# A graph attention and GCN kernel: first quotients, early loads, last stores and the last result block rearranged at the change of stage

## The chip, the core and the metric

The kernel runs on one core of one Trainium2 chip. The metric is device time in microseconds of one execution of the whole program. Engines are called as in the profile: PE is TensorE (PEld its weight loads), DVE is VectorE, ACT is ScalarE, POOL is GpSimd, and SP issues most of the transfers. A name with q behind it (SPq, ACTq, POOLq) is that engine's queue when it issues a transfer. All data is float32.

## What is computed

Two layers on N = 2708 nodes with D = 128 features and an adjacency matrix adj of 2708 x 2708. The first is an attention with 8 channels per score and one head per feature, in which the adjacency is added to the scores twice:

```
q, k, v = (x @ W.T).reshape(d, n, h)          # h = 8, d = 128 heads
a   = softmax(q @ k.T * scale + adj + adj)    # for each of the 128 heads, 2708 x 2708
out = (a @ v).reshape(n, h * d) @ Wo.T
x   = layernorm(x + out)
```

The second is a graph convolution with a residual path:

```
hidden = adj @ (x @ W2) + b2
cross  = adj @ (hidden @ W4) + b4
x      = layernorm(x + cross + hidden @ res_w.T + res_b)
```

## The kernel before

**Attention.** The 128 heads are worked in 32 groups g of four. In a group the 2708 query columns are cut into six blocks b of 452 columns (the last has 448; `QBS`), and a block has nine steps i (`plan`). In a step, TensorE forms scores of keys against queries (line 447) into PSUM; VectorE adds the adjacency to most of them (`add_near`, line 454), and ScalarE takes the exponential (line 557). For a third of the tiles ScalarE takes the exponential of the bare scores (line 554) and GpSimd multiplies it with a stored exponential of the adjacency (line 555). TensorE then multiplies the exponentials with the values (`add_up`, lines 464 to 472) and collects nine rows per head: eight weighted sums and the sum of the weights. Those sums trail the scores by several steps. When a block's sums are complete, `hand_on` copies them out of PSUM on VectorE (line 478) and stores them to the DRAM tile `os` in four transfers (line 481), issued by SP, and for the very last block by ScalarE.

**Order.** The order of all engines is written out by hand. A planner, `interleave`, holds the cost of each piece of work and decides which of scores, sums and copies comes next; it yields one item at a time, and the loop of lines 492 to 557 emits it. SP issues the adjacency tiles in that order, some eight loads ahead. At the beginning of a step (c == 0) the loop also emits what belongs to the next group or to the next stage. In the last group, from block 1 on, that is one of six `early` loads per step (line 525): the output weights `wo`, the first 128 rows of the transposed adjacency `near0`, the first 128 rows of sums `ot0`, and `x0`, `w2` and `w4`. In the last block it is the quotient of `ot0` by its sum of weights: the reciprocal ahead of step 3 (line 529), the multiplication ahead of step 5 (line 531). In the last group `look_at_near` (line 436) adds a reduction on VectorE in three of the nine steps, the last step among them.

**The second stage, `finish`.** It begins when the attention's memory is free. GpSimd sets a few tiles (lines 602 and 603). Then 22 chunks c of 128 nodes (the last has 20) pass through: `divide` (quotients on VectorE; for chunk 0 only the reductions of line 628, since its quotients are there), `turn` (four transposes on TensorE, line 634, and a copy by ScalarE, line 636, twice), `mix` (products with `wo`, line 642), `add_x` (addition, statistics, root on ScalarE, scaling, lines 647 to 653), and `spread` (line 659), which multiplies the new features with whole rows of the adjacency, two chunks later. `load` (ot and xt) and `load_rows` (rows) fetch a few chunks ahead through SP. Ahead of the loop ScalarE's queue issues four small loads (line 677): rw and the three vectors b. After the loop come `hidden`, `hidden_values`, `collect` (lines 718 to 744) and for each of six column blocks `results` (lines 753 to 775): transposes, addition to the features, statistics, root, scaling and the store. The last column block has 148 columns: one part of 128 rows and one of 20, worked one after the other. `judge` looks whether all sums stayed in range; a branch at the end repeats the attention with row maxima if they did not.

**Completion of transfers.** Transfers issued by SP and ScalarE are counted on eight semaphores in turn. A transfer that gets a semaphore waits on its own queue until the transfer eight places before it in that turn has landed. The turn is shared by both queues.

Of the kernel before, what the change touches and what calls it, by code (L numbers as in the profile page):

```python
# [9 lines left out]
F32 = mybir.dt.float32  # L10
F32R = mybir.dt.float32r
I32 = mybir.dt.int32
AF = mybir.ActivationFunctionType
# [5 lines left out]
P = 128  # L19
H = 8  # L20
GB = 4
NB = 512
QB = 452
# [119 lines left out]
def graph_attention_gcn(ctx: ExitStack, tc: tile.TileContext, x, xT, adj, adjT, adjP, adjS,  # L143
# [10 lines left out]
    nc = tc.nc  # L154
    N, D = x.shape
    R = N * D
    NG = D // GB
# [3 lines left out]
    QBS = chunks(N, QB)  # L161
# [9 lines left out]
    const = ctx.enter_context(tc.tile_pool(name="const", bufs=1))  # L171
# [17 lines left out]
    wo = const.tile([P, H, D], F32, name="wo")  # L189
    w2, w4 = (const.tile([P, P], F32, name=f"w{i}") for i in range(2))  # L190
    near0 = const.tile([P, N], F32, name="near0")
    ot0 = const.tile([P, H + 1, P], F32, name="ot0")
    x0 = const.tile([P, D], F32, name="x0")
    o3 = os_.rearrange("e (i g) -> i e g", g=P)
    early = [(wo.rearrange("g e f -> g (e f)"), WoT), (near0, adjT[:P, :]), (ot0, o3[:P]), (x0, x[:P, :]), (w2, W2), (w4, W4)]
    assert 2 * GB * N >= P * P

    with ExitStack() as s:
# [233 lines left out]
        def look_at_near(g, b, m):  # L432

            x = TWO_EXP.index(m)
            if x % 3 == g - NG + 3:
                nc.vector.tensor_reduce(ends[:, 0, ds(b * len(TWO_EXP) + x, 1)], exp_cols[g, b, m][:, : QBS[b][1]],
                                        AX.X, ALU.min)
# [37 lines left out]
        def hand_on(g, b):  # L475
            n0, nw = QBS[b]
            o = opool.tile([P, QB], F32, tag="o", name="o")
            nc.vector.tensor_copy(o[:, :nw], acc.pop((g, b))[:, :nw])  # L478
            queue = nc.scalar if (g, b) == (NG - 1, len(QBS) - 1) else nc.sync
            for j in range(GB):  # L480
                queue.dma_start(os_[:, ds((GB * g + j) * N + n0, nw)], o[ds(32 * j, H + 1), :nw])

# [9 lines left out]
        for what, n, c, beside in interleave(plan, len(steps) // len(plan), NU, amid, bufs=5):  # L492
            if what == "amid":
                at = amid.index(n)
                jobs += project(at)
                continue
            if what == "add_up":
                g, b = divmod(n, len(QBS))
                add_up(g, b, c, where.pop((g, b, c)))
                continue  # L500
            if what == "hand_on":
                hand_on(*divmod(n, len(QBS)))
                continue
            g, b, i = steps[n]
            pieces, two, _ = plan[i]
            nw = QBS[b][1]
            if c == 1 and jobs:
                jobs.pop(0)()
            if c == 0:
                nq = (g, b + 1) if b + 1 < len(QBS) else (g + 1, 0)  # L510
                if i == 3 and nq[0] < NG:
                    load_q(*nq)

                if g + 1 < NG:
                    t = b * len(plan) + i
                    if t < 32 and t % 2 == 0:
                        load_keys(g + 1, t // 2)
                    elif t < 32 and t % 8 == 7:
                        load_values(g + 1, t // 8)
                    elif 33 <= t < 50 and t % 2:  # L520
                        order_keys(g + 1, (t - 33) // 2)
                    elif t >= 50:
                        spread_values(g + 1, t - 50)
                if g == NG - 1 and b and early:
                    nc.sync.dma_start(*early.pop(0))
                if (g, b) == (NG - 1, len(QBS) - 1) and i in (3, 5):
                    if i == 3:
                        quotient = opool.tile([P, QB], F32, tag="o", name="o")[:, :P]
                        nc.vector.reciprocal(quotient, ot0[:, H, :])
                    else:  # L530
                        nc.vector.tensor_mul(ot0[:, :H, :], ot0[:, :H, :], quotient.unsqueeze(1).to_broadcast([P, H, P]))
                last = max(loads.index((g, b, x), max(0, loaded - 40)) for x in [chunks_of(p) for p in pieces] + [-1 - two])
                while loaded < min(len(loads), last + 1 + ahead):
                    load_adj(loaded)
                    loaded += 1
                e = epool.tile([P, 8, QB], F32, tag="e", name="e")
                sp = pq.tile([P, 3, NB], F32, tag="p", name="p")
                w = ppool.tile([P, 3, QB], F32, tag="w", name="w")
                if g == 0:
                    first_exp(b, two)  # L540
                at = k = 0
            st = ps.tile([P, 2, NB], F32, tag="s", name="s")
            for r, (m, j) in enumerate(pieces[c]):
                score(st[:, r], g, b, m, j)
                where.setdefault((g, b, m), {})[j] = e, at + r
            for j in beside:
                score(sp[:, k], g, b, two, j)
                where.setdefault((g, b, two), {})[j] = w, k
                k += 1
            add_near(e, st, g, b, pieces[c], at)  # L550
            at += 2
            if c == len(pieces) - 1:
                look_at_near(g, b, two)
                nc.scalar.activation(w[:, :, :nw], sp[:, :, :nw], AF.Exp, scale=2.0)  # L554
                nc.gpsimd.tensor_mul(w[:, :, :nw], w[:, :, :nw],  # L555
                                     exp_cols[g, b, two][:, :nw].unsqueeze(1).to_broadcast([P, 3, nw]))
                nc.scalar.activation(e[:, :at, :nw], e[:, :at, :nw], AF.Exp, scale=2.0)  # L557
# [3 lines left out]
    stat = ctx.enter_context(tc.tile_pool(name="stat", bufs=4))  # L561

    rw = keep.tile([P, P], F32, name="rw")
    b2_sb, b4_sb, rb_sb, bias = (keep.tile([P, 1], F32, name=f"b{i}") for i in range(4))
    eps = keep.tile([P, 1], F32, name="eps")
    n_fine = keep.tile([1, 1], I32, name="n_fine")

# [14 lines left out]
    def finish(s):  # L582
# [90 lines left out]
        for c in (1, 2):  # L673
            load(c)
            load_rows(c)
        for t, a in ((rw, res_wT), (b2_sb, b2), (b4_sb, b4), (rb_sb, res_b)):
            nc.scalar.dma_start(t, a)
        nrow = 3
        for c in range(NM):
            if c + 3 < NM:  # L680
                load(c + 3)
            while nrow < NM and nrow <= min(c + 4, max(c + NR - 2, NR)):
                load_rows(nrow)
                nrow += 1
            if c == 1:
                spread(0, range(NK))
            turn(c, 0)
            if c > 2:
                spread(c - 2, range(3))
            turn(c, 1)  # L690
            if c > 2:
                spread(c - 2, range(3, NK))
            mix(c)
            if c == 0:
                add_x(0)
            if c + 1 < NM:
                divide(c + 1)
            if c == 0:
                divide(0)
            else:  # L700
                add_x(c)
# [51 lines left out]
        def results(k):  # L753
            n0, nw = NBS[k]
            cs, eT = block_chunks[k], embeds.pop(k)
            pe = turned.tile([P, 4, P], F32, tag="pt", name="pe")
            for c in cs:
                m0, mw = MC[c]
                nc.tensor.transpose(pe[:mw, c - cs[0], :], eT[:, ds(m0 - n0, mw)], ident)
            y, o = (two.tile([P, 4, D], F32, tag=t, name=t) for t in ("y4", "o4"))  # L760
            mv = stat.tile([P, 4, nc.vector.BN_AGGR_DIM], F32, tag="mv4", name="mv4")
            full = len([c for c in cs if MC[c][1] == P])
            parts = [(0, full, P)] + [(c - cs[0], 1, MC[c][1]) for c in cs[full:]]
            for i, n, w in parts:
                nc.vector.tensor_add(y[:w, ds(i, n), :], pe[:w, ds(i, n), :], x1[:w, ds(cs[0] + i, n), :])
                for r in range(i, i + n):
                    statistics(mv[:w, r, :], y[:w, r, :], w)
                sd, rs = (stat.tile([P, 4], F32, tag=t, name=t) for t in ("sd4", "rs4"))
                nc.scalar.activation(sd[:w, :n], mv[:w, ds(i, n), 1], AF.Sqrt, bias=eps[:w])
                nc.vector.reciprocal(rs[:w, :n], sd[:w, :n])  # L770
                for r in range(i, i + n):
                    nc.vector.tensor_scalar(o[:w, r, :], y[:w, r, :], mv[:w, r, 0:1], rs[:w, r - i : r - i + 1],
                                            ALU.subtract, ALU.mult)
                m0 = MC[cs[0] + i][0]
                nc.sync.dma_start(out[ds(m0, n * w), :].rearrange("(c p) f -> p c f", p=w), o[:w, ds(i, n), :])

        def judge():
            fine = one.tile([P, 5], F32, name="fine")
# [316 lines left out]
```

## Time and profile before

| what | us |
|---|---|
| three runs | 6856.6, 6847.54, 6854.3; median 6854.3 |
| the profiled execution | 6854.41 |
| its span, first to last instruction | 6852.6 |
| attention, until the last copy of sums (line 478) | 6541.05 |
| from there until the first sums of line 659 begin | 14.9 |
| last scaling on VectorE ends | 6847.1 |
| busy PE, DVE, ACT, POOL | 6636.6, 6114.5, 6503.0, 5789.9 |
| mean granted TensorE clock | 0.992 |

The profiled execution lies 0.1 us from the median, and its own time is 1.8 us more than its span. Busy shares are means over stages with different limits. Stretches of some microseconds are therefore read in three views: the timeline of one engine (start, duration, engine, line, operation, output and input, and in brackets the idle time before it and what ended it), the windows view (busy time of each engine in a stretch, and the granted TensorE clock as a share of full speed), and the chain of waits, which runs back from the last instruction through what released each step.

### The profile page before, as it was taken

To read this page: it belongs to the slowest core of one execution; us is meant where nothing else is said; L and a number is where in the kernel's file an instruction comes from. 1 tells how busy PE (TensorE), PEld (TensorE's weight loads), DVE (VectorE), ACT (ScalarE), POOL (GpSimd) and SP (SyncE) were. 2 spreads that over 40 slices of the span, in tenths; PEclk is the share of its full clock that TensorE was granted. 3 is DMA by queue.
4 is the path that set the end of the run, shared out by engine and by line. 5 is a ranking of instruction groups with operands and counts; after the bars stand their busy time and mean duration, and the time that the engine had idled before them with its cause. 6 is when DMAs were issued, how large, how long until landed. Compare 5 with 4: busy or idle time off the path is not lost.

```text
span 6852.6 us, 138413 instructions
## 1 busy us (share of the span) xinstructions
PE 6636.6 (97%) x50612; PEld 1985.7 (29%) x50612; DVE 6114.5 (89%) x6368; ACT 6503.0 (95%) x3660; POOL 5789.9 (84%) x2706
## 2 busy tenths in 40 slices
PE   7999999999999999999999999999999999999999
PEld 2222222222222222222222222222222222222254
DVE  6899999999999999999999999999999999999952
ACT  7999999999999999999999999999999999999920
POOL 5898988999988999989899899899998888888810
PEclk8999999999999999999999999999999999999999
DMA  8888888888888888888888888888888887777774
GB/s 245 268 248 251 255 244 240 249 244 246 249 248 253 243 252 250 249 244 248 247 247 249 246 257 248 251 244 245 245 250 243 243 245 232 229 231 227 232 252 131
DMA packets 1147712, 1665.68 MB, mean 243 GB/s; under 512 B 151376, under 2 KB 1129852, under 8 KB 1140220
## 3 DMA queue, kind: packets, MB, share of 16 engines
q1 hardware_dynamic: 1146120, 1655.82, 79.8%
q8 instruction: 401, 6.57, 0.4%
q14 instruction: 287, 2.35, 0.1%
q10 hardware_dynamic: 904, 0.94, 0.1%
HBM read 1574.37 MB, written 81.80 MB: 242 GB/s over the span
## 4 chain that ended last, share of the span: by engine, by line
PE 51%; DMA 11%; DVE 10%; POOL 9%; issue 7%; ACT 6%; SPq 6%; DVEq 0%; POOLq 0%; ACTq 0%
PE acc L472 25%; PE s L447 16%; DVE e L454 9%; POOL w L555 8%; SPq L296 3%; ACT e L557 3%; DMA col<-in_adjP 3%; DMA two<-in_adjP 3%; ACT w L554 2%; DMA ecol<-ne 2%; PE acc L464 2%; PE p L447 2%; PE acc L659 2%; PE acc L741 2%; PE s L353 1%
## 5 line engine op out<-in xcount | busy, mean ns | idle before, releaser
L555 POOL TENSOR_TENSOR w<-w,ecol 128x1356 f32<-128x1356 f32 (+1 forms) x1728 | 5348.2, 3102 | 689.4 <-ACT w L554 624.2
L454 DVE TENSOR_TENSOR e<-s,col 128x904 f32<-128x904 f32 (+1 forms) x4608 | 4816.7, 1092 | 316.0 <-PE s L447 78.2
L557 ACT ACTIVATE e<-e 128x2712 f32<-128x2712 f32 (+5 forms) x1728 | 4637.0, 2683 | 16.7 <-DVE e L454 11.3
L472 PE MATMUL acc<-e,vals 128*9 128x452 f32 x20352 | 3565.4, 546 | 0.0
L447 PE MATMUL s<-q,k 32*128 32x452 f32 x10944 | 2495.9, 461 | 123.5 <-DVE e L454 89.4
L554 ACT ACTIVATE w<-p 128x1356 f32<-128x1356 f32 (+1 forms) x1728 | 2329.0, 1348 | 14.7 <-PE p L447 9.7
L447 PEld LDWEIGHTS s<-q,k 32*128 32x128 f32 x10944 | 1004.5, 182 | 3242.1 <-DVE e L454 2858.3
L472 PE MATMUL acc<-w,vals 128*9 128x452 f32 x10368 | 1628.0, 546 | 0.0
L447 PE MATMUL p<-q,k 32*128 32x452 f32 (+1 forms) x5184 | 1321.8, 445 | 21.6 <-ACT w L554 19.1
L454 DVE TENSOR_TENSOR e<-s,two 128x904 f32<-128x904 f32 (+1 forms) x960 | 1048.6, 1092 | 104.8 <-PE s L447 67.5
L472 PEld LDWEIGHTS acc<-e,vals 128*9 128x9 f32 x20352 | 442.4, 88 | 779.9 <-issue 778.7
L447 PEld LDWEIGHTS p<-q,k 32*128 32x128 f32 x5184 | 545.6, 182 | 50.9 <-ACT w L554 43.6
L472 PEld LDWEIGHTS acc<-w,vals 128*9 128x9 f32 x10368 | 209.9, 88 | 177.7 <-issue 161.3
L271 POOL CAST k<-k_raw 128x336 fp32r<-128x336 f32 x251 | 222.5, 887 | 35.7 <-DMA q<-qs 35.7
L469 PE MATMUL acc<-e,v_first 128*32 128x452 f32 (+1 forms) x1536 | 187.4, 560 | 12.7 <-ACT e L557 0.6
L464 PE MATMUL acc<-e,v_short 128*128 128x452 f32 (+1 forms) x384 | 196.7, 594 | 0.0
L353 PE MATMUL s<-wc,xc 128*128 128x256 f32 (+1 forms) x480 | 166.6, 429 | 5.2 <-DMA wc<-in_WqT 0.5
L478 DVE COPY o<-acc 128x452 f32<-128x452 f32 x192 | 120.3, 627 | 51.1 <-PE acc L472 51.1
L355 DVE TENSOR_SCALAR pa<-s 128x256 f32<-128x256 f32 (+1 forms) x240 | 100.3, 418 | 31.8 <-PE s L353 24.9
L369 POOL TENSOR_TENSOR pr<-pa,pr 128x256 fp32r<-128x256 f32 (+1 forms) x160 | 117.6, 735 | 12.8
L353 PEld LDWEIGHTS s<-wc,xc 128*128 128x128 f32 (+1 forms) x480 | 69.5, 183 | 156.0 <-DVE e L454 153.8
L659 PE MATMUL acc<-rows,x 128*128 128x512 f32 (+2 forms) x252 | 103.1, 545 | 0.0
(90 smaller groups left out, 1031.4 us busy)
## 6 DMA issues: line engine op xcount, KB each, us to landing
col<-in_adjP SPq DMA_DIRECT2D x1965, 226.0 KB
two<-in_adjP SPq DMA_DIRECT2D x1440, 226.0 KB
ecol<-ne SPq DMA_DIRECT2D x1395, 226.0 KB
col<-in_adjP SPq DMA_DIRECT2D x393, 224.0 KB
two<-in_adjP SPq DMA_DIRECT2D x288, 224.0 KB
ecol<-ne SPq DMA_DIRECT2D x279, 224.0 KB
k_raw<-ks SPq DMA_DIRECT2D x504, 84.6 KB
two<-in_adjS SPq DMA_DIRECT2D x160, 226.0 KB
```

The source lines that it names most:

```text
L271: copy(k[:, :, ts(i, n)], t[:, ts(i, n * NU)].rearrange("p (q c) -> p c q", c=NU))
L296: queues[i].dma_start(q[ds(32 * j + 2 * H * i, 2 * H), :nw].bitcast(F32), qs[:, ds((GB * g + j) * N + n0, nw)])
L353: nc.tensor.matmul(pp[:mi, 0, :QW], given[c][:, :mi], given.pop((c, i, h)), start=True, stop=True)
L447: nc.tensor.matmul(to[:, :nw], k[r, m, :], q[r], start=True, stop=True)
L454: nc.vector.tensor_add(e[:, ds(at, 2), :nw], st[:, :, :nw], a)
L464: nc.tensor.matmul(a[:, :nw], vz, e[:, t, :nw], start=False, stop=False)
L469: nc.tensor.matmul(a[ds(32 * j, 32), :nw], v_first[g % 2][:, ds(32 * j, 32)], e[:, t, :nw], start=True, stop=False)
L472: nc.tensor.matmul(a[ds(32 * j, VW), :nw], v[:, m, ds(VW * j, VW)], e[:, t, :nw], start=False, stop=(m == last_chunk))
L554: nc.scalar.activation(w[:, :, :nw], sp[:, :, :nw], AF.Exp, scale=2.0)
L555: nc.gpsimd.tensor_mul(w[:, :, :nw], w[:, :, :nw], exp_cols[g, b, two][:, :nw].unsqueeze(1).to_broadcast([P, 3, nw]))
L557: nc.scalar.activation(e[:, :at, :nw], e[:, :at, :nw], AF.Exp, scale=2.0)
L659: nc.tensor.matmul(accs[k][:, :nw], x1[:mw, m, :], rows[m][:mw, ds(n0, nw)], start=(m == 0), stop=(m == NM - 1))
```

## The change

It touches four places. (1) In the last group, `early` loads are given out at every second step of all blocks, and are cut up: `near0` into six pieces by columns, `ot0` into three by rows of sums, `wo` into two; the three b vectors, now kept in the constant pool, join them, which makes 17. rw is loaded by SP at c = 5 of the second stage. (2) The reciprocal and the multiplication for `ot0` are emitted behind the last step's addition and reduction. (3) The last sums' four stores are issued by GpSimd. (4) In `results` the additions of both parts come first, then both statistics and roots, then both scalings; the 128-row parts are stored by ScalarE's queue, the 20-row part by SP.

```diff
@@ the tiles and early loads
+    b2_sb, b4_sb, rb_sb, bias = (const.tile([P, 1], F32, name=f"b{i}") for i in range(4))
     o3 = os_.rearrange("e (i g) -> i e g", g=P)
-    early = [(wo.rearrange("g e f -> g (e f)"), WoT), (near0, adjT[:P, :]), (ot0, o3[:P]), (x0, x[:P, :]), (w2, W2), (w4, W4)]
+    early = [(near0[:, ds(n0, nw)], adjT[:P, ds(n0, nw)]) for n0, nw in QBS]
+    early += [(ot0[:, ds(3 * i, 3), :], o3[:P, ds(3 * i, 3)]) for i in range(3)]
+    early += [(wo.rearrange("g e f -> g (e f)")[:, ts(i, NB)], WoT[:, ts(i, NB)]) for i in range(2)]
+    early += [(x0, x[:P, :]), (w2, W2), (w4, W4), (b2_sb, b2), (b4_sb, b4), (rb_sb, res_b)]
@@ hand_on
-            queue = nc.scalar if (g, b) == (NG - 1, len(QBS) - 1) else nc.sync
+            queue = nc.gpsimd if (g, b) == (NG - 1, len(QBS) - 1) else nc.sync
@@ the loop over the plan
-                if g == NG - 1 and b and early:
+                if g == NG - 1 and i % 2 and early:
                     nc.sync.dma_start(*early.pop(0))
-                if (g, b) == (NG - 1, len(QBS) - 1) and i in (3, 5):
-                    if i == 3:
-                        quotient = opool.tile([P, QB], F32, tag="o", name="o")[:, :P]
-                        nc.vector.reciprocal(quotient, ot0[:, H, :])
-                    else:
-                        nc.vector.tensor_mul(ot0[:, :H, :], ot0[:, :H, :], quotient.unsqueeze(1).to_broadcast([P, H, P]))
...
                 look_at_near(g, b, two)
+                if n == len(steps) - 1:
+                    quotient = opool.tile([P, QB], F32, tag="o", name="o")[:, :P]
+                    nc.vector.reciprocal(quotient, ot0[:, H, :])
+                    nc.vector.tensor_mul(ot0[:, :H, :], ot0[:, :H, :], quotient.unsqueeze(1).to_broadcast([P, H, P]))
                 nc.scalar.activation(w[:, :, :nw], sp[:, :, :nw], AF.Exp, scale=2.0)
@@ finish
-        for t, a in ((rw, res_wT), (b2_sb, b2), (b4_sb, b4), (rb_sb, res_b)):
-            nc.scalar.dma_start(t, a)
...
+            if c == 5:
+                nc.sync.dma_start(rw, res_wT)
@@ results
             for i, n, w in parts:
                 nc.vector.tensor_add(y[:w, ds(i, n), :], pe[:w, ds(i, n), :], x1[:w, ds(cs[0] + i, n), :])
+            sds, rss = (stat.tile([P, 4], F32, tag=t, name=t) for t in ("sd4", "rs4"))
+            for i, n, w in parts:
                 for r in range(i, i + n):
                     statistics(mv[:w, r, :], y[:w, r, :], w)
-                sd, rs = (stat.tile([P, 4], F32, tag=t, name=t) for t in ("sd4", "rs4"))
-                nc.scalar.activation(sd[:w, :n], mv[:w, ds(i, n), 1], AF.Sqrt, bias=eps[:w])
-                nc.vector.reciprocal(rs[:w, :n], sd[:w, :n])
+                nc.scalar.activation(sds[:w, ds(i, n)], mv[:w, ds(i, n), 1], AF.Sqrt, bias=eps[:w])
+            for i, n, w in parts:
+                nc.vector.reciprocal(rss[:w, ds(i, n)], sds[:w, ds(i, n)])
                 for r in range(i, i + n):
-                    nc.vector.tensor_scalar(o[:w, r, :], y[:w, r, :], mv[:w, r, 0:1], rs[:w, r - i : r - i + 1],
+                    nc.vector.tensor_scalar(o[:w, r, :], y[:w, r, :], mv[:w, r, 0:1], rss[:w, r : r + 1],
                                             ALU.subtract, ALU.mult)
                 m0 = MC[cs[0] + i][0]
-                nc.sync.dma_start(out[ds(m0, n * w), :].rearrange("(c p) f -> p c f", p=w), o[:w, ds(i, n), :])
+                (nc.sync if i else nc.scalar).dma_start(out[ds(m0, n * w), :].rearrange("(c p) f -> p c f", p=w), o[:w, ds(i, n), :])
```

On TensorE the built program has the same order as before. On VectorE two instructions move. On GpSimd the four stores stand last, behind the tiles that it sets for the second stage.

## Prediction

> **What bounds the kernel now.** I read the page's chain of waits first: up to 6541 us it alternates between TensorE, VectorE, ScalarE and GpSimd, and after 6563 it is almost all TensorE. So I cut the end of the run into stretches by the windows view (columns: stretch, then busy us and count of PE, PEld, DVE, ACT, POOL, then granted TensorE clock, DMA share, GB/s). Three rows at an ordinary block boundary of the last group, then four in its last block:
>
> ```profile
> 6402.00:6404.00 2.00, 1.81 (x17) 0.38 (x13) 1.71 (x3) 2.00 (x3) 2.00 (x1) 1.00 0.02 5
> 6404.00:6406.00 2.00, 1.02 (x11) 0.45 (x13) 2.00 (x3) 2.00 (x2) 2.00 (x2) 1.00 0.00 0
> 6406.00:6408.00 2.00, 2.00 (x20) 0.49 (x12) 2.00 (x3) 2.00 (x3) 1.84 (x2) 1.00 0.20 45
> ...
> 6506.00:6508.00 2.00, 0.77 (x5) 0.50 (x5) 2.00 (x4) 1.83 (x1) 2.00 (x1) 0.72 0.00 0
> 6508.00:6510.00 2.00, 2.00 (x11) 0.28 (x10) 1.70 (x2) 1.51 (x2) 1.08 (x2) 0.50 0.11 24
> 6516.00:6518.00 2.00, 1.21 (x14) 0.21 (x12) 2.00 (x3) 2.00 (x2) 1.73 (x1) 1.00 0.52 196
> 6522.00:6524.00 2.00, 2.00 (x19) 0.60 (x15) 0.86 (x2) 2.00 (x1) 1.95 (x1) 0.50 0.00 0
> ```
>
> An ordinary block is bound by ScalarE: busy 33.66 of 33.8 us in 6404.9 to 6438.7. In the last block the clock is 0.50 from 6506.9 to 6513.7 and from 6520.5 to 6527.2; TensorE then is busy all the time and ScalarE only 24.32 of 34.0 us. What stands ahead of both slow stretches is in VectorE's timeline (start, duration, engine, line, operation):
>
> ```profile
> 6504.76 0.61 DVE L436 TENSOR_REDUCE ends<-ecol 128x1 f32<-128x448 f32 x1
> 6505.28 0.94 DVE L529 RECIPROCAL o<-ot 128x128 f32<-128x128 f32 x1
> 6506.14 1.03 DVE L454 TENSOR_TENSOR e<-s,col 128x896 f32<-128x896 f32 x1
> 6507.09 0.61 DVE L478 COPY o<-acc 128x452 f32<-128x452 f32 x1
> ...
> 6515.64 1.22 DVE L531 TENSOR_TENSOR ot<-ot,o 128x1024 f32<-128x1024 f32 x1
> ```
>
> The quotient of rows 0 to 127 delays two additions for which TensorE waits. The reciprocal makes its wait 1.86 us, where other boundaries have 1.07. Then the change of stage, in ScalarE's timeline (a bracket is the idle time before):
>
> ```profile
> 6541.05 0.36 ACTq L677 DMA_DIRECT2D rw<-in_res_wT  x1
> 6541.45 0.44 ACTq L677 DMA_DIRECT2D b<-in_b  x1
> 6541.99 1.86 ACTq L481 DMA_DIRECT2D os<-o  x4
> 6543.89 0.37 ACTq L677 DMA_DIRECT2D b<-in_b  x1
> 6548.25 0.37 ACTq L677 DMA_DIRECT2D b<-in_res_b  x1
> 6548.71 0.58 ACT L636 COPY oT<-pt 128x512 f32<-128x512 f32 x1 [10.45 <-DMA os<-o]
> ```
>
> The copy of chunk 0's first transposes, which TensorE finished at 6541.55, stands behind eight transfers. The view puts its wait down to os; the built program says more: completions are counted on eight semaphores in turn, and the res_b load has the one of the rw load, so ScalarE stands until rw has landed at 6548.2. Finally the last block of results on VectorE: its 20-row part starts only when the 128-row part is done.
>
> ```profile
> 6845.12 0.35 DVE L772 TENSOR_SCALAR o<-y,mv,rs 128x128 f32<-128x128 f32 x1
> 6845.38 0.27 DVE L765 TENSOR_TENSOR y<-pe,x 20x128 f32<-20x128 f32 x1
> 6846.78 0.33 DVE L772 TENSOR_SCALAR o<-y,mv,rs 20x128 f32<-20x128 f32 x1
> ```
>
> **What the Trainium skill says.** "TensorE: Matmul & The Clock Gate", Part 1: the array runs at half rate after a quiet window of about 3.4 us and at full rate after a busy one, and the window is "free-running". The trace agrees with the two rates and the window: 0.50 or 1.00, slow stretches of 3.4 us (6336.2 to 6339.6) or 6.8. It differs on the idle needed: 1.07 us of waiting at a boundary was enough twice in this group and not three times. "DMA: Bandwidth & Descriptors", Queues, rings and completion order: each engine works off its ring in order and takes the queues in turn by packets. That fits rw: 64 KB issued 0.02 us after 1,354 KB of rows took 7.2 us. Same page, Anatomy of one DMA — SWDGE (gpsimd) path: a fixed 2.0 us for a transfer from GpSimd. No transfer from GpSimd is in this trace.
>
> **The change, part by part.** The profiled execution took 6854.41 us, its span 6852.6; the median of the three runs is 6854.3, so the sum made against the profile stands for the median within 0.1. The three spread over 9 us.
>
> (1) Quotient moved behind VectorE's last addition. It removes 0.86 us (6505.28 to 6506.14) and 1.13 us (6515.64 to 6516.77) from VectorE inside the block. Block ends, by the copies of line 478, are 33.83 us apart twice (6404.85, 6438.68, 6472.51); the next took 34.58. So this copy comes at 6472.51 + 33.83 = 6506.34 instead of 6507.09. Then I lay block 4 over block 5: there ScalarE's last e ends 24.78 us after the copy (6497.29 - 6472.51), with columns 448/452 as wide 24.56; 6506.34 + 24.56 = 6530.9, against 6538.27. After it the sums of the last step and their copy took 2.78 us (to 6541.05), which I keep: 6533.7. Cross-check: from the last scores (6533.7) TensorE works 7.3 us without a break; block 4 has its last scores 20.0 us after its copy, so 6526.1 + 7.3 = 6533.4. Gain 7.3. If the window happens to fall badly at this boundary, one slow stretch stays; blocks 0 and 1, which have one, took 35.42 and 35.38, so it costs 1.6. The quotient's new place: VectorE is idle for 5.84 us ahead of the last copy, and 0.94 + 1.22 us fit in. The first transposes now wait for it, 4 us after it is done. Without that cover it would cost 2.1.
>
> (2) The last sums' stores (4 issues, 1.86 us) go to GpSimd, the b loads (3) to SP in blocks 3 and 4, rw (1) to SP at c = 5. ScalarE's queue is empty at the change of stage; its copy then waits for the transposes and old column loads. From the start of the transposes (6540.89): 0.66 for four of them, copy until 1.3, four more until 2.0, products 2.0 to 3.8 (1.78 as in later chunks; here 3.4 at half clock), then to the first sums of line 659 the 2.0 us of today (6553.9 to 6555.91: addition, statistics, root, reciprocal, scaling). That is 5.85 us, against 15.02 today: 9.2. Those twelve matmuls took 7.56 us, mostly at half clock; at full clock it is 2.58 + 1.97 = 4.55. The 2.0 us of idle remain, so I expect one to two slow stretches and count 0.8 of the 3.0. Sum 10.0, ends 8 and 12.2. What is late next: SP's second ot load had waited from 6541.4 to 6548.06 for the semaphore of the rows load; without the eight transfers in between it has another, and follows at once. At the 400 GB/s of this stretch rows 1 (1.39 MB) and ot 2 (0.59 MB) land some 9 us after the transposes start, and chunk 2 needs it after 15. On GpSimd the stores stand behind five memsets (0.1 to 0.2 us each, before them in the built order), with nothing behind them. They are read 150 us later. I price them at nothing; a GpSimd queue in the program may cost up to 2.0 us (the skill's fixed cost, taken as the upper end), and cannot gain. rw is one more 0.4 us issue on SP, some 140 us ahead of its use.
>
> (3) Early loads: 6 transfers of up to 1,354 KB become 17 of at most 256 KB, on SP behind every second step of blocks 0 to 4. Blocks 0 and 1 look 1.6 us longer than 2 and 3, but each has one slow stretch, which begins at 6336.2, before the first early load (6346.27). What loads cost there is one wait of 0.18 us for a col tile on VectorE. Gain 0.2, ends 0 and 3.2. New issues on SP (11 of 0.4 us over 170 us) fit between its waits.
>
> (4) Last block side by side: the 20-row addition and statistics (0.27, 0.28, 0.17) run while ScalarE takes the 128-row root. The start gaps of today give: 128 rows scaled 6845.38 to 6845.73, 20 rows 6845.82 to 6846.15, against 6847.11. Gain 0.95; both stores go on separate queues, and what follows the last one (5.5 us) stays.
>
> (5) Stores of the other blocks move from SP to ScalarE (5 issues): TensorE runs without a gap there (line 741), so 0. ScalarE has about 20 us between roots.
>
> Sum: 7.3 + 10.0 + 0.2 + 0.95 = 18.45; 6854.4 - 18.45 = 6836.
>
> **Rivals.** A: the sum, 6836, own range 6831 to 6840. B: the slow clock of the last block stays, since TensorE waits on VectorE elsewhere in it, and only VectorE's 2.0 us come back. For it: two other boundaries of equal waits went slow. Against: none of the five other blocks has a second slow stretch in its middle. 7.3 becomes 2.0: 6841. C: ScalarE is free but the loads are late, chunk 2 or 3 waiting for ot. For it: rows 1 took 7.03 us to land. Against: 15 us are there and 9 needed. Half of the 10.0 goes: 6841. D: slower. Each early piece delays the column loads behind it until TensorE's wait crosses the window's limit, 1.6 us a piece. 17 pieces give 27 - 18.4 = 9 more: 6863; it turns slower than before once 12 of the 17 do it. Against: the two largest loads together caused 0.18 us of waiting. That the change doesn't do what it says is excluded by the built order, save for pools: the stores are last on GpSimd, the quotient is behind the last addition.
>
> **How the numbers follow.** Chances: A 0.70, B 0.13, C 0.13, D 0.04. A measurement of this kernel can tell about 0.2% (13.7 us) from no change: faster is below 6840.6, slower above 6868. A is nearly all below; B and C straddle the bound, 0.45 of each; so faster 0.69 + 0.12 = 0.81, slower 0.02 of D, within 0.17. Range: slow stretches at boundaries come and go by 1.6 us each, and the full 12.2 with 3.2 for loads is the lower end, 6830; B and C together with the 2.0 of GpSimd's queue give the upper, 6846.
>
> **What would show it.** Right: clock 1.00 from the last boundary to the last copy, about 27 us apart; the transposes' copy within 1 us of them; TensorE idle for 2 to 3 us instead of 10 around the change of stage; the last scaling done 3.4 us after the last eT began. Wrong: idle on ScalarE over 3 us in the last block, an ot load that TensorE waits for, a column load waited for behind the pieces.

## The result, and the profile after

| | us |
|---|---|
| changed kernel, median of 20 runs | 6846.27 (6835.01 to 6852.78) |
| kernel before, median of 20 runs | 6855.53 (6841.41 to 6863.85) |
| ratio, 95% interval | 0.9985 [0.9978, 0.9992] |
| the changed kernel's profiled execution, its span | 6849.71, 6847.9 |

The change is faster by 9.3 us in the medians; by the interval by 5.5 to 15 us. The prediction said 18.45 us. The direction is right, the size is half. Its own bound for "faster", below 6840.6 us, to which it gave a chance of 0.81, was not reached.

The windows of the changed kernel come first (same columns as before): three rows at the boundary ahead of the last two blocks, three in the last block, and the change of stage.

```profile
6478.00:6480.00 2.00, 0.82 (x10) 0.35 (x7) 2.00 (x4) 2.00 (x2) 2.00 (x2) 1.00 0.00 0
6480.00:6482.00 2.00, 2.00 (x13) 0.38 (x13) 2.00 (x3) 2.00 (x2) 2.00 (x1) 0.51 0.15 32
6484.00:6486.00 2.00, 2.00 (x13) 0.41 (x10) 0.86 (x2) 0.90 (x1) 1.61 (x1) 0.50 0.90 271
...
6516.00:6518.00 2.00, 1.38 (x13) 0.45 (x13) 2.00 (x3) 2.00 (x2) 2.00 (x2) 1.00 0.06 13
6518.00:6520.00 2.00, 2.00 (x20) 0.60 (x20) 2.00 (x3) 2.00 (x3) 1.82 (x2) 1.00 0.11 20
6528.00:6530.00 2.00, 2.00 (x21) 0.48 (x21) 2.00 (x3) 2.00 (x2) 1.49 (x1) 1.00 0.00 0
...
6548.00:6550.00 2.00, 0.46 (x1) 0.30 (x2) 1.50 (x5) 0.29 (x1) 0.00 (x0) 1.00 0.91 336
6550.00:6552.00 2.00, 2.00 (x6) 0.95 (x5) 1.97 (x5) 0.00 (x0) 0.00 (x0) 1.00 1.19 379
```

The last block runs at full clock with ScalarE busy in every row; the change of stage runs at full clock too. But one block earlier, where no quotient stands, an ordinary boundary went slow for 7 us. Next VectorE's timeline around the last copy of sums (now line 482):

```profile
6516.48 0.62 DVE L482 COPY o<-acc 128x452 f32<-128x452 f32 x1
6537.92 0.94 DVE L554 RECIPROCAL o<-ot 128x128 f32<-128x128 f32 x1
6538.90 4.09 DVE L555 TENSOR_TENSOR ot<-ot,o 128x1024 f32<-128x1024 f32 x1
6543.84 0.62 DVE L482 COPY o<-acc 128x448 f32<-128x448 f32 x1 [0.85 <-PE acc L476]
```

From copy to copy 27.36 us (27.4 predicted), against 33.96. ScalarE's timeline at the change of stage has no transfer left in it; the copy starts 0.7 us after the transposes begin (6543.68) instead of 7.8:

```profile
6538.65 2.44 ACT L559 ACTIVATE e<-e 128x2688 f32<-128x2688 f32 x1
6544.37 0.59 ACT L637 COPY oT<-pt 128x512 f32<-128x512 f32 x1 [3.28 <-PE pt L635]
6545.70 0.59 ACT L637 COPY oT<-pt 128x512 f32<-128x512 f32 x1 [0.74 <-PE pt L635]
```

The first sums of `spread` (line 660 now) begin at 6549.54, 5.86 us after the transposes began (5.85 predicted, 15.02 before). In the last block of results both parts run side by side on VectorE:

```profile
6839.50 0.37 DVE L752 TENSOR_SCALAR eT<-acc,b 128x148 f32<-128x148 f32 x1 [1.00 <-PE acc L745]
6841.92 0.34 DVE L775 TENSOR_SCALAR o<-y,mv,rs 128x128 f32<-128x128 f32 x1
6842.36 0.33 DVE L775 TENSOR_SCALAR o<-y,mv,rs 20x128 f32<-20x128 f32 x1
```

So the places that the prediction named did what it said, but for the boundary one block earlier. In these two executions the places gave even more than forecast: group 31's six blocks 7.5 us, from the last copy to the first row sums 11.9, the end 1.4, together 20.8. (The first row sums stand in chunk 3's pass, two chunks behind their rows; they are called chunk 3's below.) Yet the spans differ by 4.7 only. Some 16 us are lost elsewhere: 10.3 are already lost at the copy of group 30's last sums (6344.35 against 6334.05), ahead of nearly all that the change does; 1.1 behind the change of stage; and 4.8 where the stage of sums hands over to `hidden`. The largest single piece of the first is one late column tile in mid-attention (VectorE):

```profile
5415.18 1.10 DVE L458 TENSOR_TENSOR e<-s,two 128x904 f32<-128x904 f32 x1 [3.45 <-DMA two<-in_adjP]
```

TensorE waited 3.0 us for this addition and then ran at half clock for 10.2 us; that block took 39.56 us, where the same block in the 13 other profiles took 33.2 to 34.1. Does the change cause such losses, or does chance? That is what the experiments are about.

### The profile page after: what moved, and what is told of

Same layout as the page of the kernel before. It is cut to its first block, busy times and chain, and to the rows that moved or that the text cites. A ratio compares the mean times of both kernels' runs of the same rounds, so it can differ in the third digit from the quotient of the medians.

```text
span 6847.9 us, 138426 instructions
## 1 busy us (share of the span) xinstructions
PE 6633.7 (97%) x50612; PEld 1982.5 (29%) x50612; DVE 6117.5 (89%) x6368; ACT 6504.6 (95%) x3660; POOL 5791.3 (85%) x2710
## 4 chain that ended last, share of the span: by engine, by line
PE 46%; DMA 16%; DVE 9%; POOL 9%; issue 7%; SPq 7%; ACT 6%; DVEq 0%; POOLq 0%; ACTq 0%
PE acc L476 22%; PE s L451 14%; DVE e L458 8%; POOL w L557 8%; DMA col<-in_adjP 6%; SPq L300 4%; DMA two<-in_adjP 3%; ACT e L559 3%; DMA ecol<-ne 3%; ACT w L556 3%; PE acc L468 2%; PE acc L660 2%; PE acc L742 2%; PE p L451 1%; DMA k_raw<-ks 1%
```

## The experiments

Kernels that were timed together share the runs of the kernel before. Of each there is one profiled execution, called its profile. A ratio stands beside its 95% interval. Three theories: "chance", that slow stretches of the clock fall now here, now there, and one profile oversized the gain; "loads", that the finish runs into its own loads; and, formed on the way, "place", that the four tiles b2, b4, res_b and bias, which the change puts in the first pool, move all tiles of the attention by 128 bytes and that this costs time.

**The two large parts alone.** e1_quotient is the kernel before with only the quotient moved, e2_queue with only ScalarE's queue emptied:

```diff
e2_queue, against the kernel before
+    b2_sb, b4_sb, rb_sb, bias = (const.tile([P, 1], F32, name=f"b{i}") for i in range(4))
...
-    early = [..., (w2, W2), (w4, W4)]
+    early = [..., (w2, W2), (w4, W4), (b2_sb, b2), (b4_sb, b4), (rb_sb, res_b)]
...
-            queue = nc.scalar if (g, b) == (NG - 1, len(QBS) - 1) else nc.sync
+            queue = nc.gpsimd if (g, b) == (NG - 1, len(QBS) - 1) else nc.sync
...
-    b2_sb, b4_sb, rb_sb, bias = (keep.tile([P, 1], F32, name=f"b{i}") for i in range(4))
...
-        for t, a in ((rw, res_wT), (b2_sb, b2), (b4_sb, b4), (rb_sb, res_b)):
-            nc.scalar.dma_start(t, a)
...
+            if c == 5:
+                nc.sync.dma_start(rw, res_wT)
```

> The kernel before with one part of the change: chunk 0's quotient behind VectorE's last addition; the whole early loads and ScalarE's queue at the change of stage are as before. Sum of the prediction: 7.3 us faster than the kernel before, with the last two blocks' slow stretches of the clock gone and the last boundary to the last copy in 27.4 us instead of 34. Rival 'chance': the slow stretches beside the quotient are not in every execution of the kernel before, and the median moves by 4 us or less, though the profile shows the block at 27.4. Rival 'slow clock stays': the last block takes 32 us, median 2 us faster.

Measured: 6848.07 us (13 runs; before 6853.63), 0.9996 [0.9988, 1.0005]. The profile has the last two blocks at 33.78 and 27.36 us. The interval, 8 us faster to 3 slower, fits a gain of 4 to 5 and just leaves 7.3 possible.

> The kernel before with another part alone: b2, b4 and res_b loaded early, rw from SyncE's queue at chunk 5, the last sums stored by GpSimd's queue, so that ScalarE copies the first transposes at once. Sum of the prediction: 10.0 us faster. What the two profiles show: 10.8 from the last copy of sums to chunk 4's first sums (15.02 to 5.86 us up to the first of the 12 sums, 2.7 from the clock, 1.1 given back where chunk 4 waits for its ot). Rival 'loads bound': with the quotient unmoved TensorE still runs into loads, 6 us or less. Without the slow stretches of the last block removed, the last copy stays where it was before.

Measured: 6847.54 us (13 runs), 0.9996 [0.9988, 1.0005]: at most 8 us faster, while its own trace has 5.85 us from the transposes to the first sums and 18.65 us from the last copy to chunk 3's row sums, where the six profiles with ScalarE's old queue have 29.5 in the mean. Its last blocks, with the quotient in the old place, tell what the quotient costs without a slow stretch (VectorE):

```profile
6505.88 0.94 DVE L530 RECIPROCAL o<-ot 128x128 f32<-128x128 f32 x1
6507.68 0.62 DVE L479 COPY o<-acc 128x452 f32<-128x452 f32 x1
6513.41 1.22 DVE L532 TENSOR_TENSOR ot<-ot,o 128x1024 f32<-128x1024 f32 x1
6536.16 0.62 DVE L479 COPY o<-acc 128x448 f32<-128x448 f32 x1 [5.83 <-PE acc L473]
```

28.48 us from copy to copy, 1.12 over the 27.36; the block ahead took 34.58, 0.80 over 33.78. The clock was 1.00 in both blocks. So the quotient itself costs 1.9 us, and the rest of the 7.4 that the first profile showed were slow stretches, which came with it there.

**The early loads, both ways.** e3_whole is the changed kernel with whole early loads from block 1 on; e5_pieces the kernel before with the loads cut up (14 pieces, `i % 2` for `b`).

> The changed kernel with its early loads undone: whole tensors, from group 31's second block on, as before. Sum of the prediction: the pieces are worth 0.2 us (0 to 3.2), so the same as the changed kernel within 3.2 us. Rival 'pieces cost': each of the 17 loads holds SyncE's queue and column loads come late; then this kernel is faster than the changed one by several us, and blocks of group 31 take less than 33.9 us each.

> The kernel before with one part of the change: its early loads in 14 small pieces over all blocks of group 31. Sum of the prediction: 0.2 us faster (0 to 3.2). Theory now ('slow stretches come by chance of the clock's windows'): no difference in the mean; and the profile, a second look at the end of the kernel before, shows less than the 20 us that the first one lost from the last two blocks to chunk 3 (last two blocks 34.58 and 33.96 us, last copy to first sums 14.86, first sums to chunk 3's 15.71). Rival 'the old end always loses this much': the four numbers come again within 1 us.

Measured: e3_whole 6842.11 us (17 runs), 0.9983 [0.9975, 0.9990]; e5_pieces 6854.13 us (13 runs; before 6855.37), 0.9999 [0.9991, 1.0008]. Pieces change nothing that can be measured. In the profiles, blocks 0 to 3 of group 31 lose 0 to 3.2 us to slow stretches with either kind: 2.2 in the mean of eight with whole loads, 1.7 in six with pieces. e5_pieces also profiles the old end once more: its blocks took 37.62 and 31.51 us, off by 3.0 and 2.5, but the four numbers add to 99.05 us as in the first profile (99.11). "Chance" in its plain form is wrong there: slow stretches shift, and most of them come.

**Loads at the change of stage.** In the changed kernel chunk 4's quotient stood waiting for its ot on VectorE:

```profile
6563.67 0.35 DVE L654 TENSOR_SCALAR x<-y,mvs,rs 128x128 f32<-128x128 f32 x1
6568.02 0.95 DVE L626 RECIPROCAL rd<-ot 128x128 f32<-128x128 f32 x1 [4.01 <-DMA ot<-os]
```

SyncE's queue at that time: its small xt loads hold it for 3 to 6 us each, where in the kernel before most took 1 us or less.

```profile
6556.15 0.38 SPq L612 DMA_DIRECT2D ot<-os  x1
6556.57 6.37 SPq L614 DMA_DIRECT2D xt<-in_x  x1
6562.99 0.43 SPq L620 DMA_DIRECT2D rows<-in_adjT  x1
6563.53 0.38 SPq L612 DMA_DIRECT2D ot<-os  x1
6564.01 4.39 SPq L614 DMA_DIRECT2D xt<-in_x  x1
```

The first two such loads (6544.67 and 6549.12) wait for no semaphore in the trace, so none holds them; the queue seems to take no more while several MB are on their way, which is not shown. ot 4 was issued at 6556.15 behind rows 3 and 4, 1,354 KB each. e4_order asks for rows later:

```diff
e4_order, against the changed kernel
-        for c in (1, 2):
-            load(c)
-            load_rows(c)
-        nrow = 3
+        load(1)
+        load(2)
+        load_rows(1)
+        nrow = 2
...
-            while nrow < NM and nrow <= min(c + 4, max(c + NR - 2, NR)):
+            while nrow < NM and nrow <= c + 2:
```

> The changed kernel with the finish's loads in another order: each chunk's row load two chunks ahead of its use instead of four, so that ot of chunk 4 stands behind one row load less. If the late load of chunk 4 is all that the change of stage loses, TensorE's wait of 1.1 us before chunk 4's sums goes, and the time falls by 1.1 us, which the profile shows and the median of 20 hardly does. Rival 'loads bound': the whole finish runs behind its loads, and several us come back. Rival: row loads now come late themselves, and sums wait for rows.

Measured: 6844.5 us (16 runs), 0.9985 [0.9978, 0.9993]. In its profile no quotient up to chunk 5's waits for an ot, and the xt loads from chunk 4's on hold the queue for 0.6 to 1.2 us; from chunk 3's to chunk 4's row sums it takes 7.21 us, the steady period, where the changed kernel took 8.29. So 1.1 us is all that "loads" can claim; the median can't tell it. Nor was it won in this profile: a slow stretch of 3.4 us fell into the twelve sums (6.51 us instead of 4.81), and from the last copy to the first product with w2 it took 164.1 us, where the changed kernel took 163.5. The three later kernels with this order have such a stretch too; so has e3_whole, which has the old one, so the order isn't shown to bring it.

**The last block alone, and the old end again.** e6_side is the kernel before with the last block's parts side by side and nothing else of the change; e8_again is the kernel before unchanged, one profile and no other run.

> The kernel before with another part alone: the last block's statistics, scalings and stores side by side on two queues. Sum of the prediction: 0.95 us faster; the last copy of the embedding to VectorE's end falls from 4.35 to 3.2 us and nothing else moves. A third look at the old end: by 'chance' the two last blocks and the change of stage take other times than in the first look by several us; by 'always' they come again within 1 us.

> The kernel before once more, unchanged, for one more look at its end. 'Chance': last two blocks and change of stage differ from the first look by several us, up to 10 us less in all. 'Always': 34.58, 33.96, 14.86 and 15.71 us again within 1 us.

Measured: e6_side 6852.25 us (13 runs), 0.9997 [0.9988, 1.0005]; from the last eT to VectorE's end 3.19 us instead of 4.35, and to the end of the span 8.0 instead of 9.9. e8_again's one execution took 6859.51 us; its last blocks took 34.58 and 33.91 us, the change of stage 14.97 and 12.96. TensorE's timeline of e8_again there:

```profile
6543.20 0.66 PE L634 MATMUL pt<-ident,ot 128*128 128x128 f32 x4
6551.77 1.11 PE L634 MATMUL pt<-ident,ot 128*128 128x128 f32 x4 [7.91 <-ACT oT L636]
6552.68 3.62 PE L642 MATMUL py<-wo,oT 128*128 128x128 f32 x16
6558.33 4.81 PE L659 MATMUL acc<-near,x 128*128 128x512 f32 x12 [2.03 <-DVE x L653]
```

The wait of 7.9 us is the same; the twelve sums, 7.56 us in the first profile, ran at full clock here. So 2.7 us of that profile were chance, the rest was not.

**The handover.** Between the first product with w2 and the first product of the second layer that reads a column tile (`near`), 16.30 us in some profiles are 21.1 in others. The windows of the changed kernel there:

```profile
6706.00:6708.00 2.00, 2.00 (x7) 0.85 (x6) 0.15 (x2) 0.59 (x1) 0.00 (x0) 1.00 0.00 0
6708.00:6710.00 2.00, 2.00 (x4) 0.59 (x3) 0.28 (x1) 0.00 (x0) 0.00 (x0) 0.68 0.03 8
6712.00:6714.00 2.00, 2.00 (x6) 0.64 (x4) 0.38 (x1) 0.00 (x0) 0.00 (x0) 0.50 0.00 0
```

TensorE is busy in every row, as this view counts it, and the clock still falls to half. Among what it works on are the products of the last chunk, which has 20 rows. e7_fill sets the last sums of 128 rows between them (and has e4_order's loads and whole early loads):

```diff
e7_fill, the handover
-        spread(NM - 2, range(NK))
+        spread(NM - 2, [5, 4, 3])
...
         take(5)
+        spread(NM - 2, [2])
         spread(NM - 1, [3])
         take(4)
         hidden(5)
+        spread(NM - 2, [1])
         spread(NM - 1, [2])
         hidden(4)
         take(3)
+        spread(NM - 2, [0])
```

> The changed kernel with whole early loads, the mended load order, and the sums of the last full chunk set between the sums of the 20-row chunk, so that TensorE has a 128-row product beside each 20-row one where the stage of sums hands over. 'Chance' and the handover: three of six profiles so far lost 4.8 us to a slow stretch of three windows there (16.30 us to the second stage's column products without, 21.1 with); mixed with full products it is gone in this look, and the mean falls by about 2 us against the changed kernel. Rival 'the handover's slow stretch is of another cause': 21 us again, no gain.

Measured: 6843.19 us (21 runs), 0.9983 [0.9976, 0.9990]. One slow window of 3.4 us was still there; from chunk 3's row sums to the first column product it took 162.1 us, against 160.1 in undisturbed profiles and 164.9 in e8_again and e1_quotient, which have three slow windows there. No gain is shown. What all profiles together say of the cause stands in the last section.

**The place of the tiles.** f1_shift is the kernel before with only the four tiles moved; f2_back is the changed kernel with them moved back (b2, b4, res_b then loaded at chunk 5 with rw):

```diff
f1_shift, against the kernel before
+    b2_sb, b4_sb, rb_sb, bias = (const.tile([P, 1], F32, name=f"b{i}") for i in range(4))
...
-    b2_sb, b4_sb, rb_sb, bias = (keep.tile([P, 1], F32, name=f"b{i}") for i in range(4))
```

> The kernel before, with only the place of b2, b4, res_b and bias changed: the four one-column tiles stand in the first pool instead of the one opened after the attention, so that every tile of the attention lies 128 bytes further on; they are loaded when and where they were. 'Place': the five profiles with these tiles in the first pool end group 31's first block at 6340.2 us in the mean (6333.5 to 6345.4), the five without at 6334.9 (6333.0 to 6337.0), so the place costs the attention some 5 us: mean of the runs 5 us over the kernel before. 'Chance': late column loads that fall as they will; mean within 2 us of the kernel before.

> The changed kernel with the four tiles back in the later pool, so that the attention's tiles lie where the kernel before has them; b2, b4 and res_b are loaded by SyncE's queue behind rw at chunk 5. 'Place': the parts measured in the traces (quotient 5.0, change of stage 8.9, last block 1.5) come out undiminished: 15 us faster than the kernel before. 'Chance': as the changed kernel, 10 us faster.

Measured: f1_shift 6855.96 us (13 runs; before 6852.90), 1.0004 [0.9995, 1.0012]; f2_back 6842.64 us (21 runs), 0.9983 [0.9977, 0.9990]. What the expectation calls the end of group 31's first block is the copy of group 30's last sums; f1_shift has it at 6329.0, the earliest of all profiles, against "place". Undecided, so once more as a pair, with e4_order's loads in both: h1_best with the tiles back, h2_moved with them in the first pool.

> The changed kernel with both mends: the four one-column tiles back in the later pool, and each chunk's row load two chunks ahead instead of four. Against the kernel before: the traces' parts (quotient 4.9, change of stage 10.0 without a wait for ot, last block 1.4) are 16 us. 'Place' says 13 us or more faster; 'chance' says as the changed kernel and its mends so far, 10 to 12 us.

> The kernel of the run before this one, with the four tiles in the first pool again and nothing else, so that every tile of the attention lies 128 bytes further on. 'Place' says 3 to 5 us slower than the other, and its profile may end group 31's first block at 6340 us or later; 'chance' says the same mean within 2 us.

Measured: h1_best 6835.19 us (7 runs only; before 6854.17), 0.9971 [0.9960, 0.9982]; h2_moved 6843.2 us (19 runs), 0.9985 [0.9978, 0.9992]. The three pairs give 2.7, 1.4 and 9.6 us by their ratios, all to the disadvantage of the moved tiles, each with an uncertainty of 5 us or more; the two intervals of the last pair overlap a little. In the profiles, the copy of group 30's last sums comes at 6339.1 in the mean with moved tiles (6329.0 to 6345.4) and at 6335.9 without (6333.0 to 6341.7). A cost of some 4 us is likely; it is not shown, and how 128 bytes would cost it was not found. Moves by 64 and 512 bytes, which would tell, were not tried. One rival runs through all these kernels: storing the last sums from GpSimd, for which the prediction allowed up to 2.0 us. The same copy comes at 6340.1 in the mean of the eight profiles with those stores (6333.5 to 6345.4) and at 6333.9 in the six without (6329.0 to 6337.0), so it splits the profiles more widely than the place does. Within each pair it is the same, so the pairs test the place alone; no kernel has GpSimd's stores and nothing else, and their cost is untested. h1_best, with f2_back's and e4_order's edits on the changed kernel, is the fastest of this study, 19 us below the kernel before in the medians and 8 below h2_moved, though on few runs.

All profiles side by side, in us, worked out from the traces. A star marks moved tiles; "copy" is that of group 30's last sums, "last two" group 31's last two blocks, "change" from the last copy to chunk 3's first row sums, "to handover" from there to the first product with w2, "handover" from there to the first product with a column tile, "end" from the last eT to the end of the span.

| profile | copy | last two | change | to handover | handover | end |
|---|---|---|---|---|---|---|
| before | 6334.1 | 68.5 | 30.6 | 143.8 | 16.3 | 9.9 |
| e8_again | 6336.7 | 68.5 | 27.9 | 143.8 | 21.1 | 9.5 |
| e5_pieces | 6337.0 | 69.1 | 29.9 | 143.8 | 16.3 | 9.8 |
| e6_side | 6333.9 | 69.1 | 30.3 | 143.8 | 16.3 | 8.0 |
| f1_shift* | 6329.0 | 65.7 | 29.7 | 143.8 | 18.0 | 9.2 |
| e1_quotient | 6333.0 | 61.1 | 28.5 | 143.8 | 21.1 | 9.7 |
| e2_queue* | 6335.0 | 63.1 | 18.7 | 144.9 | 21.1 | 9.7 |
| changed kernel* | 6344.4 | 64.1 | 18.7 | 144.8 | 21.1 | 8.4 |
| e3_whole* | 6333.5 | 61.1 | 20.4 | 144.2 | 18.0 | 8.3 |
| e4_order* | 6345.4 | 61.2 | 20.4 | 143.8 | 16.3 | 8.3 |
| e7_fill* | 6343.0 | 65.7 | 20.4 | 142.4 | 19.7 | 8.3 |
| f2_back | 6334.7 | 61.1 | 18.7 | 144.5 | 22.7 | 8.2 |
| h1_best | 6341.7 | 61.1 | 20.4 | 143.8 | 16.3 | 8.4 |
| h2_moved* | 6343.5 | 65.7 | 20.4 | 143.8 | 18.0 | 8.3 |

## Why the prediction was right in direction and wrong in size

**(1) The quotient, 7.3 forecast.** The mechanism is right: out of the block it is gone, and a clean block takes 27.36 us. The size is the term "7.3", taken from one execution. Over six profiles with the quotient in the old place the last two blocks took 67.3 us in the mean, not 68.5; over eight with it in the new place 62.7, not the clean 61.1, since three of them have a slow stretch of their own at the boundary ahead, and two of these a last block longer by 1.5. 4.7 us remain. The prediction booked that stretch as "if the window happens to fall badly" at 1.6 us and outside its sum; it costs 3.0 to 4.5 in three of eight profiles. Its cover for the quotient's new place was wrong too, though this cost nothing: the multiplication took 4.1 us there, not 1.22, and was done 0.7 us before the transposes, not 4. Rival B (slow clock of the last block stays, 2.0) is refuted by the five clean profiles.

**(2) The emptied queue, 10.0 forecast.** The largest term is exact: 5.86 us for 5.85. The change of stage takes 29.5 us in the mean of six old profiles and 19.7 in eight new ones: 9.8. The prediction expected one to two slow stretches in it; three of the eight have none, five have one. Behind it late ot loads take 0.4 to 1.1 (mean 0.8 in the four profiles with the change's load order), which leaves 8.9 net. Rival C had the right thing and the wrong size: chunk 4 waits, not 2 or 3, and 1.1 us of the 10 go, not 5. "ot 2 lands some 9 us after the transposes" was no false step: VectorE began chunk 2's quotient when ot 2 had landed, 9.8 us after them, and TensorE did not wait for it. But the step looked no further than chunk 2, and the load that came late stood two chunks on.

**(3) The pieces, 0.2 forecast.** Right: no difference in the time. Rival D, 1.6 us for each piece, is refuted by e5_pieces: 14 pieces would cost 22 us, and its interval ends at 5.5 slower.

**(4) Side by side, 0.95 forecast.** 1.4 in the profiles (9.6 to 8.3 us from the last eT to the end): 1.16 on VectorE and some 0.2 behind it.

**(5) Other stores: 0.** Nothing in the traces speaks against it, for those that moved to ScalarE.

**What failed.** The parts come to 4.7 + 8.9 + 1.4 = 15.0 us by the profiles, the medians to 9.3, and the interval's upper end is 15. The step that failed, as far as the runs show it, is the quotient's term: it took all slow stretches of one profiled execution for the quotient's own and gave the new place none, 7.3 us where 4.7 were measured. In all, 3.4 us of the forecast 18.45 were mis-sized terms.

Some 5.7 us more are not in the trace of the places at all, unless the true gain lies at the interval's end. The sum priced only the places where instructions move: it has no term for the four tiles that the change puts into the first pool, and it priced the queue of GpSimd's stores at nothing. The three pairs make some 4 us of the first likely; the second was not tested. The handover is 1.0 us longer in the profiles with an emptied queue than without; with 16.3 and 21.1 us in both groups that is within chance. Whether place, GpSimd's stores or chance holds the 5.7 can't be settled with these runs.

**The range** of the prediction, 6830 to 6846, came from the bounds of the terms. It left out that executions of the same kernel lie 22 and 18 us apart in the two sets of 20 runs. The measured median, 6846.27, lies at its upper end.

## What to carry to other kernels

One profiled execution is enough to find a wait and to size it when the wait is structural: 5.85 us were forecast and 5.86 came. It isn't enough to size slow stretches of the clock: they shift from boundary to boundary with any shift of a few us ahead of them (the next section shows the grid that they lie on), so take their mean over several executions, and give the new place the same chance of them as the old one. When a change touches a memory pool that is opened first, look at what moves behind it, and time that move by itself.

## What the runs showed of the hardware

**Where slow stretches fall.** In each of the 14 profiles every change of the clock lies on one grid with a step of 3.413 us, to within 0.003 us over the whole span. At the six block boundaries from the end of group 30 to the start of group 31's last block, 84 in all profiles, TensorE waits for VectorE's addition: 1.05 to 1.07 us at 78 of them, about 1.86 where the reciprocal stands ahead. Where the short wait straddled two windows of the grid, none of 42 was followed by a slow stretch; where it lay inside one window, 21 of 36 were. Of the six long waits four were. So what the experiments call chance is in good part where a boundary falls on the grid, and anything that shifts the boundaries by a few us deals the slow stretches anew. What decides between the 21 and the other 15 is not settled.

**The handover.** There the clock of the changed kernel was 0.50 for 10.2 us with TensorE counted busy in every window, so a slow stretch doesn't need a wait that the profile shows. Laid on the same grid, the 14 profiles part cleanly: in nine of them the last chunk's sums, products of 20 rows, filled 2.12 us or more of a window at full clock, and the next window was slow; in the five others they never filled more than 2.08 us, and none was. That makes the 20-row products the likely cause. It was read from the traces after the runs; no kernel without such products was timed, and e7_fill, which only moved them apart, still had one window with 2.24 us.

**VectorE beside GpSimd.** The multiplication of the quotient took 1.22 us in its old place and 4.06 to 4.09 us in the new one, in all six and all eight profiles. In the new place GpSimd's product began first (6538.83 to 6541.90 in the changed kernel) and VectorE's, begun at 6538.90, ended 1.09 us after it; in the old place VectorE's began first (6515.64) and GpSimd's, begun at 6516.27, took 3.51 us instead of 3.1. The Trainium skill, "SBUF — State Buffer", Summary: rules for kernel authors, says that where a VectorE instruction has two SBUF inputs and GpSimd's reads SBUF, the second one to issue "fully blocks" until the first finishes. The trace agrees in the new place, and roughly in the old one (an overlap of 0.6 us made GpSimd's product 0.4 us longer). This ate 2.9 of the 4 us that the prediction had as cover.
